# Which engine copies the carry column of a scan tile: ScalarE for two tiles of three instead of one

## The chip, the cores and the metric

The kernel runs on one core of a Trainium2 chip. The core has a matrix engine (TensorE, PE in the profile), three engines for elementwise work (VectorE = DVE, ScalarE = ACT, GpSimd = POOL) and a queue engine (SyncE = SP) that issues its transfers. Each engine works through its own list of instructions in order and waits on semaphores for the others. The metric is the device time of one execution in microseconds (us), lower is better. Before the change it is 11125.21 us, the median of three runs (11121.33 to 11125.94).

## The reference

The input is 8 images of 64 x 64 pixels with 96 channels. Two layers are computed one after the other, each added to its input. The first is a selective scan block: group norm, a projection to 192 channels, a 3x3 depthwise convolution with SiLU, then a recurrence along the 4096 pixels in four directions, and at the end a norm, a gate and an output projection. The second is a small MLP between an upsampling and a downsampling filter. Nearly all of the time goes to the recurrence:

```
def step(h, inp):
    ul, dl, Bl, Cl = inp                       # one pixel
    dA = jnp.exp(dl[..., None] * A)            # 4 directions x 192 channels x 16 states
    h = dA * h + (dl * ul)[..., None] * Bl[:, :, None, :]
    y = jnp.einsum('bkdn,bkn->bkd', h, Cl)
    return (h, y)
_, ys = lax.scan(step, h0, (u_t, d_t, B_t, C_t))
```

## The kernel before, in words

**Tiles.** A tile holds 8 channels x 16 states on the 128 partitions and T = 1024 pixels along the free axis. For an image and a direction k the 4096 pixels are cut into NCH = 4 chunks, and each chunk has NT = 24 tiles, one for each group g of 8 channels. That makes 8 x 4 x 4 x 24 = 3072 tiles. They are worked off in one long loop, chunk after chunk, the 24 groups of a chunk one behind the other.

**A tile's work.** `product_b` (L1069, always GpSimd) forms the input term bb. `decay` (L1071 to L1082) has TensorE spread dl over the states into a PSUM tile pd (four matmul rows of the profile, L1075), and ScalarE takes the exponential of pd in place (L1082). `scan` (L1089, VectorE) runs the recurrence through the tile. `product_c` (L1095) multiplies the result by C, and `sums` (L1127) has TensorE add over the states.

**Thirds.** Tiles are dealt out by i % 3, where i counts the 24 tiles of a chunk. A tile with i % 3 == 2 is "GpSimd's" (`by_pool`): its scan writes to a tile h in SBUF, and GpSimd forms its product. The other two thirds scan in place in PSUM, and VectorE forms their product. In this text tile 0, tile 1 and tile 2 are the tiles of the three residues, and tile 0' is the tile 0 that follows tile 2.

**The carry.** The scan of a chunk starts from the last column of the same group in the chunk before. `hold` (L1104) therefore copies one column of the finished tile (the last one, or the first one for the backward directions) into column g of a small tile `carry`. The last chunk of a direction needs no copy, so three tiles of four have one: 2304 copies in all. Before the change ScalarE copies for tiles 2, from SBUF, and VectorE for tiles 0 and 1, from PSUM.

**Buffers.** pd has two buffers (L232). The matmuls of tile n + 2 therefore wait until everything that reads the pd of tile n is done: its scan alone for a tile 2, its product and its copy for tiles 0 and 1.

**Order.** The order on every engine is written out by hand in the loop: in the step of tile n come the product of tile n - 1 if it is GpSimd's, `product_b` for tile n + 3, `decay` for tile n + 1, the scan of tile n, its product if VectorE's, its copy, then a portion of side work (`side.advance`: the convolutions, norms and the MLP of neighbouring images, rationed by `Side.CAPS`, L49), a filler matmul if PE has little to do (`turn_over`, L1097), and every second step the sums. So on ScalarE the list reads: exp of tile n + 1, copy of tile n if it is ScalarE's, side work, exp of tile n + 2, and so on.

Of the kernel before, what the change touches and what calls it, by code (L numbers as in the profile page):

```python
# [136 lines left out]
def kernel(ctx: ExitStack, tc: tile.TileContext, a: dict, out: bass.AP):  # L137
    nc = tc.nc
# [965 lines left out]
    def hold(t):  # L1104
        if t["last"]:
            return
        end = T - 1 if t["k"] < 2 else 0
        (nc.scalar.copy if t["by_pool"] else nc.vector.tensor_copy)(  # L1108
            carry[:, t["g"] : t["g"] + 1], t["h"][:, end : end + 1]
        )  # L1110

# [60 lines left out]
    with tc.manual_schedule():  # L1172
# [20 lines left out]
        for i in range(n + 4):  # L1193
            t = tiles[i] if i < n else None
# [48 lines left out]
            if t:  # L1243
                scan(t)
                if not t["by_pool"]:
                    product_c(t)
                hold(t)
# [105 lines left out]
```

## Time and profile before

| what | us |
|---|---|
| median of three runs | 11125.21 |
| the profiled execution | 11107.68 |
| its span (first to last instruction) | 11105.8 |
| busy: VectorE / GpSimd / TensorE / ScalarE | 10207.5 / 10179.6 / 9967.9 / 5910.6 |
| stretch 125 to 10835 us, in which the scans run | 10710, VectorE busy 10157.2, GpSimd 10147.7 |
| VectorE's 3072 scans, about 2.3 each | 7164 |
| VectorE's 2048 products (1.225 each), GpSimd's 1024 (2.357 each) | 2508.4 and 2413.9 |
| VectorE's 1536 copies, 0.148 each | 228.0 |
| ScalarE's 768 copies, 0.183 each | 140.8 |

A row of the profile such as "L1108 DVE COPY carry<-pd" names the source line, the engine, the operation and what it writes and reads. Busy times are sums over the rows of one engine; two rows that follow each other closely can overlap by some 0.08 us, since the next instruction starts before the one before has fully ended. A line of the waits names the instruction that waited, what released it, the total in us, the number of times and the longest.

### The profile page before, as it was taken

What the parts mean: (1) busy time and instruction counts of PE and PEld (TensorE: products, weight loads), DVE (VectorE), ACT (ScalarE), POOL (GpSimd) and SP (SyncE); (2) the same over time, 40 slices, a digit from 0 to 9 for tenths busy, and PEclk for the clock granted to TensorE, in tenths of its full rate; (3) what the DMA queues carried; (4) which work ended last, traced back from release to release, by engine and by line L of the source; (5) the groups of instructions that cost most, each with busy time, mean ns of one, the idle gap of its engine ahead of it and who ended that gap; (6) DMA issues with size and microseconds to landing.
All of it is one profiled execution on the core that took longest, in us unless ns stands there. A gap on an engine that the chain in (4) does not pass through costs nothing. (4 is left out here: it accounts for less than half of the span.)

```text
span 11105.8 us, 137238 instructions
## 1 busy us (share of the span) xinstructions
PE 9967.9 (90%) x45020; PEld 3204.6 (29%) x45020; DVE 10207.5 (92%) x7702; ACT 5910.6 (53%) x8218; POOL 10179.6 (92%) x4674
## 2 busy tenths in 40 slices
PE   8898888989889998999889998899988989889988
PEld 2222222322233222332223322233222332223325
DVE  6999999999999999999999999999999999999990
ACT  5455445656455564555545555455554655545543
POOL 5999999999999999999999999999999999999990
PEclk9999999999999999999999999999999999999998
DMA  6888898898988989888988989889898898988981
GB/s 174 215 208 224 209 231 209 217 227 232 233 209 216 225 231 225 212 218 224 240 217 215 224 221 244 209 219 225 217 243 210 217 228 218 247 206 216 227 214 48
DMA packets 1044463, 2401.27 MB, mean 216 GB/s; under 512 B 293820, under 2 KB 314556, under 8 KB 1043752
## 3 DMA queue, kind: packets, MB, share of 16 engines
q1 hardware_dynamic: 1042776, 2391.45, 86.5%
q8 instruction: 361, 5.91, 0.2%
q14 instruction: 350, 2.87, 0.1%
q10 hardware_dynamic: 976, 1.04, 0.0%
HBM read 1929.05 MB, written 328.73 MB: 203 GB/s over the span
## 5 line engine op out<-in xcount | busy, mean ns | idle before, releaser
L1069 POOL TENSOR_TENSOR bb<-dub,br 128x1024 f32<-128x1024 f32 x3072 | 7173.5, 2359 | 208.4 <-DMA dub<-du 149.2
L1082 ACT ACTIVATE pd<-pd,neg_a 128x1024 f32<-128x1024 f32 x3072 | 3340.7, 1088 | 4533.0 <-PE pd L1075 4489.8
L1075 PE MATMUL pd<-dl,sel_b 64*128 64x512 f32 x12288 | 3512.7, 645 | 987.2 <-DVE carry L1108 649.2
L1089 DVE TENSOR_TENSOR_SCAN pd<-pd,carry,bb 128x1024 f32<-128x1024 f32 x1536 | 3610.3, 2350 | 262.2 <-ACT carry L1108 127.9
L1095 POOL TENSOR_TENSOR hc<-h,cr 128x1024 f32<-128x1024 f32 x1024 | 2413.9, 2357 | 352.6 <-DVE h L1089 300.7
L1095 DVE TENSOR_TENSOR hc<-pd,cr 128x1024 f32<-128x1024 f32 x2048 | 2508.4, 1225 | 164.1 <-PE py L1127 20.0
L1075 PEld LDWEIGHTS pd<-dl,sel_b 64*128 64x128 f32 x12288 | 966.7, 186 | 3266.3 <-issue 1511.2
L1089 DVE TENSOR_TENSOR_SCAN h<-pd,carry,bb 128x1024 f32<-128x1024 f32 x768 | 1797.3, 2340 | 5.8 <-ACT pd L1082 5.6
L1127 PE MATMUL py<-hc,sel_r 128*32 128x512 f32 x12288 | 1715.0, 617 | 30.4 <-POOL hc L1095 30.2
L1089 DVE TENSOR_TENSOR_SCAN pd<-pd,bb 128x1024 f32<-128x1024 f32 x512 | 1172.5, 2290 | 98.6 <-ACT carry L1108 75.3
L1101 PE MATMUL idle<-sel_b,ident 128*128 128x512 f32 x1652 | 932.0, 646 | 8.0 <-DVE ty L720 5.9
L562 PE MATMUL pc<-pad,convr 96*128 96x512 f32 (+1 forms) x2304 | 858.3, 616 | 5.7 <-DVE e L585 3.6
L1089 DVE TENSOR_TENSOR_SCAN h<-pd,bb 128x1024 f32<-128x1024 f32 x256 | 583.6, 2280 | 26.0 <-ACT pd L1082 25.2
L1127 PEld LDWEIGHTS py<-hc,sel_r 128*32 128x32 f32 x12288 | 250.3, 109 | 1109.0 <-issue 854.5
L1031 POOL TENSOR_TENSOR u<-dl,u 128x512 f32<-128x512 f32 x384 | 485.0, 1271 | 79.2 <-DVE dl L1028 79.2
L862 PEld LDWEIGHTS p<-w2q,mq 128*100 128x100 f32 x4800 | 452.9, 168 | 274.6 <-issue 214.2
L855 PE MATMUL ph<-xu,w 96*128 96x500 f32 x960 | 504.9, 629 | 11.5 <-ACT mq L856 6.7
L862 PE MATMUL p<-w2q,mq 128*100 128x96 f32 x4800 | 511.5, 258 | 2.3 <-ACT mq L856 2.3
L562 PEld LDWEIGHTS pc<-pad,convr 96*128 96x128 f32 (+1 forms) x2304 | 266.3, 163 | 563.9 <-issue 552.8
L987 PE MATMUL px<-u,xp 64*64 64x512 f32 x1536 | 422.4, 627 | 2.4 <-issue 2.4
L1101 PEld LDWEIGHTS idle<-sel_b,ident 128*128 128x128 f32 x1652 | 249.8, 189 | 596.5 <-issue 522.4
L1012 PE MATMUL pv<-xd,dt_w 64*64 64x512 f32 x1536 | 394.4, 609 | 1.0 <-ACT xd L997 1.0
(153 smaller groups left out, 6707.9 us busy)
## 6 DMA issues: line engine op xcount, KB each, us to landing
dub<-du SPq DMA_DIRECT2D x3072, 512.0 KB
u<-u SPq DMA_DIRECT2D x256, 384.0 KB
du<-u SPq DMA_DIRECT2D x768, 128.0 KB
y<-yq SPq DMA_DIRECT2D x768, 128.0 KB
br<-xd SPq DMA_DIRECT2D x256, 256.0 KB
cr<-xd SPq DMA_DIRECT2D x256, 256.0 KB
yp<-y SPq DMA_DIRECT2D x384, 128.0 KB
yp<-u SPq DMA_DIRECT2D x192, 128.0 KB
```

The lines of the kernel that those rows point to most:

```text
L562: nc.tensor.matmul(t[rows].rearrange("p (i j) -> p i j", i=8), weights[:, cs], v["pad"][:, 8 * blk + kw : 8 * blk + kw + 8, kh : kh + H], ...
L855: nc.tensor.matmul(t[:, :px], w1[:, m, :], xu, start=True, stop=True)
L862: nc.tensor.matmul(t[:SIDE, C * i : C * i + C], sq[:, m, row], w2q[:, m, :], start=(m == 0), stop=(m == 2))
L987: nc.tensor.matmul(p[rows], xp[rows, k, q, :], v["u"][rows, q, :], start=(q == 0), stop=(q == 2), skip_group_check=True,)
L1031: nc.gpsimd.tensor_tensor(v["u"][:, q, :], got["dl"][:, q, :], v["u"][:, q, :], ALU.mult)
L1069: nc.gpsimd.tensor_tensor(t["bb"], t["dub"], t["got"]["br"], ALU.mult)
L1075: nc.tensor.matmul(pd[:, MB * hf : MB * hf + MB], sel_b[rows, 4 * t["s"] + t["j"]].rearrange("p n c -> p (n c)"), t["got"]["dl"][rows, t[" ...
L1082: nc.scalar.activation(pd, pd, AF.Exp, scale=neg_a[:, t["k"], t["g"] : t["g"] + 1])
L1089: nc.vector.tensor_tensor_scan(t["h"][:, ::step], pd[:, ::step], t["bb"][:, ::step], 0.0 if t["first"] else held, ALU.mult, ALU.add)
L1095: (nc.gpsimd if t["by_pool"] else nc.vector).tensor_tensor(t["hc"], t["h"], t["got"]["cr"], ALU.mult)
L1101: nc.tensor.matmul(p, ident, sel_b[:, 0:4].rearrange("p j n c -> p (j n c)"), start=True, stop=True)
L1127: nc.tensor.matmul(py[r0 : r0 + 32], sel_r[:, t["j"], :], t["hc"][:, MB * hf : MB * hf + MB], start=(t["j"] == 0), stop=(t["j"] == 3 and t ...
```

## The change

`hold` chooses its engine by the tile's place instead of by `by_pool`. Tiles 2 stay on ScalarE and tiles 0 on VectorE; the copies of tiles 1 (768 of them), which read pd in PSUM, move from VectorE to ScalarE. The blank line moves all later source lines by one.

```
-        (nc.scalar.copy if t["by_pool"] else nc.vector.tensor_copy)(
+
+        (nc.vector.tensor_copy if t["i"] % 3 == 0 else nc.scalar.copy)(
             carry[:, t["g"] : t["g"] + 1], t["h"][:, end : end + 1]
         )
```

In the list of the changed program's instructions, with the semaphore value that each waits for, three more things differ. The moved copy waits on ScalarE until VectorE has finished `product_c` of tile 1, not only its scan. The matmuls of tile 0' wait for ScalarE's copy where they waited for VectorE's. And the exp of tile 0' has a second wait, for the copy, in 621 of 768 cases behind its wait for the matmuls.

## The prediction

> **What bounds the kernel now.** I read the page's busy times first, then the copy's own rows and who waited for them, then VectorE's waits, then one group of three tiles in order of time. From the page:
>
> ```profile
> PE 9967.9 (90%) x45020; PEld 3204.6 (29%) x45020; DVE 10207.5 (92%) x7702; ACT 5910.6 (53%) x8218; POOL 10179.6 (92%) x4674
> ```
>
> VectorE and GpSimd share the lead, ScalarE is half idle. By that line alone, moving work from VectorE to ScalarE looks free. The rows of line 1108 say who is held up by the copy:
>
> ```profile
> L1108 DVE COPY carry<-pd x1536: 146/148/151, 123.6 to 10750.5; 128x1 f32<-128x1 f32 x192
> L1108 ACT COPY carry<-h x768: 172/182/193, 133.1 to 10754.4; 128x1 f32<-128x1 f32 x192
> ...
>   PE pd L1075: 649.2, 796
> ```
>
> TensorE's decay matmuls waited 796 times for a copy: it stands on the way to releasing a pd buffer. The waits tell which of the two leaders drives:
>
> ```profile
> DVE pd L1089 <- ACT carry L1108: 203.2, 414, 3.6
> ...
> POOL hc L1095 <- DVE h L1089: 300.7, 335, 6.4
> ...
> DVE pd L1089 <- ACT pd L1082: 113.8, 238, 8.0
> ...
> DVE pd L1089 <- POOL bb L1069: 40.2, 38, 2.3
> ```
>
> GpSimd waits 300.7 us for VectorE's scans, VectorE only 40.2 us for GpSimd, so VectorE sets the pace. Its own large waits are before in-place scans, for ScalarE. The line names the copy, but the order of time shows that the exp in front of it is meant (the chain of tiles 1, 2 and 0'):
>
> ```profile
> 5013.53 1.22 DVE L1095 TENSOR_TENSOR hc<-pd,cr 128x1024 f32<-128x1024 f32 x1
> 5014.67 0.15 DVE L1108 COPY carry<-pd 128x1 f32<-128x1 f32 x1
> 5014.74 2.34 DVE L1089 TENSOR_TENSOR_SCAN h<-pd,carry,bb 128x1024 f32<-128x1024 f32 x1
> ...
> 5014.97 1.13 PE L1075 MATMUL pd<-dl,sel_b 64*128 64x512 f32 x4 [1.31 <-DVE carry L1108]
> ...
> 5016.13 1.09 ACT L1082 ACTIVATE pd<-pd,neg_a 128x1024 f32<-128x1024 f32 x1 [2.77 <-PE pd L1075]
> ...
> 5017.15 0.18 ACT L1108 COPY carry<-h 128x1 f32<-128x1 f32 x1
> ...
> 5017.32 2.36 DVE L1089 TENSOR_TENSOR_SCAN pd<-pd,carry,bb 128x1024 f32<-128x1024 f32 x1 [0.24 <-ACT carry L1108]
> ```
>
> Product 1 ends at 5014.75, copy 1 at 5014.82, the matmuls of tile 0' run 5014.97 to 5016.10, its exp to 5017.22, and scan 0' starts 0.10 later. Meanwhile VectorE finished scan 2 at 5017.08 and stood idle. So from product 1 to scan 0' there are two ways: VectorE's own (copy, scan 2) and a chain through TensorE and ScalarE, and the chain is longer by about 0.3 us. Counted over the trace: of the 768 groups of three with copies, 485 have scan 0' starting within 0.13 us of its exp's end. In these the chain decides; in the other 283 side work of VectorE or something else does.
>
> **The change, part by part.** The sum is made for the profiled execution (11107.7 us, span 11105.8) and carried to the median of the runs, which is 17.5 us higher.
>
> *Removed from VectorE:* 768 copies. One does not cost its 0.148: it starts 0.084 before the product's end, and the scan starts 0.083 before the copy's end, where without a copy (tile pairs of the last chunks) the scan starts 0.084 before the product's end. Each costs 0.064, together 49 us. That is the most that can be gained, and only where VectorE's own way is the longer one.
>
> *Added to ScalarE:* 768 copies from PSUM. The row for SBUF is 0.183. ScalarE's 96x1 activations take 0.249 from PSUM (L493) and 0.203 from SBUF (L494), so PSUM adds 0.046; I take 0.230, with 0.183 as the lower end.
>
> *The new wait.* The copy waits for product 1. ScalarE's copies that waited for a scan of VectorE began 0.034 after its end (121 cases). Released are the matmuls of tile 0'. In the chunks without copies, matmuls with a single wait began 0.054 after the product (118 cases); a matmul of L855 that waited for ScalarE began 0.052 after it (12 cases). So product to matmuls takes 0.034 + 0.230 + 0.052 = 0.316. Before, it was 0.210 in the common form with two waits (407 cases) and 0.119 with one (58). Then the exp: with its matmul wait alone or last it follows the matmuls by 0.039 to 0.048, but the exps of tiles 1 that carry a second wait behind it followed by 0.108 (249 cases). 621 exps of tile 0' get this form: +0.069. Together the chain grows by 0.106 + 0.069 = 0.175 us in the common case, 0.13 with the shorter copy.
>
> The Trainium skill, "PSUM — Partial Sum Buffer", section "PSUM bank collisions raise a hardware error", speaks against the change: two engines may not touch one bank and quadrant at the same time, readers included, and the back end orders them. That is a reason why a copy that needs only scan 1 is put behind product 1, which reads the same tile; no row of the trace before shows two engines reading one pd. Were copy and product allowed side by side, the sum would be the first rival's below.
>
> Term 1: of the 485, 412 have no further trouble (next paragraph). I put each exp where the new chain ends and compared with the old start of scan 0'. The mean is 0.150, as some matmuls were late already because of TensorE's own list: **+61.7 us** (+50.0 with the short copy).
>
> *What is queued behind the waiting copy.* ScalarE's list is exp 2, copy 1, side work, exp 0'. Before, the side work could start when exp 2 ended, at the median 1.12 us before product 1's end, and had some 3.6 us. Now it starts after the copy, and exp 0' is ready 0.052 + 1.129 + 0.108 = 1.29 us later. Side work there: median 0.60 us, 90% point 1.90, over 1.3 in 138 of 768 groups (sigmoids L506 to L511, squares L856, the Ln and Exp of L1024 and L1026). With each instruction overlapping the one before by 0.075, the exp is late in 130 groups, by 0.60 at the mean. In 73 of them the chain decided before: +0.73 each with the 0.175 included, 53.3 us. In 57 there was slack: +0.28 each, 16.0 us. Term 2: **+69.3 us** (+63.9).
>
> Term 3: in the remaining 226 groups VectorE's own way decides or the slack swallows the delay: **-10.4 us** (-11.9) by the missing copies.
>
> *Hidden parts.* The second semaphore of scan 0' (for product 1) is met 2.3 us early and costs nothing as long as scan 2 lies between. ScalarE has the time: 53% busy, and 768 x 0.230 is 177 us. Tiles 0 and 2 and their releases stay as they are, and no transfer is issued or moved. GpSimd comes later with VectorE; its 300.7 us of waiting grows.
>
> Sum: 61.7 + 69.3 - 10.4 = **+120.6 us** (+102 with the short copy; +79.7 if the exp's second wait also costs nothing; +153.3 if ScalarE's signal reaches TensorE as slowly as the 0.146 seen in the two-wait form). 11107.7 + 120.6 = 11228 for the profiled run, **11245 us** on the median.
>
> **Rivals.**
> *1. The copy runs beside the product (faster).* Scan 1 ends 1.26 us before product 1. A copy released then is done early, the matmuls follow product 1 by 0.054 instead of 0.210, and VectorE saves 0.064. It decides if copies start before the product's end. Price: 485 x 0.156 + 283 x 0.064 = -94, given back 485 x 0.069 for the second wait: -60, so about 11065. Against it stands the wait in the instruction list.
> *2. The chain alone.* If side work on ScalarE has found its place in other gaps, Term 2 shrinks to the 0.175 for its 73 groups: 61.7 + 12.8 - 10.4 = +64, so 11189. For it: ScalarE is idle 4490 us before exps. Against it: that idle time lies before exp 0' no longer, since the copy cuts it off.
> *3. The late side work spreads.* TensorE's next side matmuls read what ScalarE wrote late, and the matmuls of tile 1' stand behind them; exps of tile 1 have a median slack of 0.73 before their scan. If the overrun of 130 x 0.60 = 77 us is paid once more, the sum is +198 and the time 11323.
> *4. No change.* Stalls of other origin (POOL 40.2 us and TensorE's list) take up the delay and the copy is short: within 22 us of 11125.
>
> **Chances.** Forecast (+80 to +155) 0.60, rival 3 and beyond 0.17, rival 2 0.14, rival 1 0.04, rival 4 0.05. The range takes the forecast, rival 2 and rival 3 to a little beyond its price: 11170 to 11335. About 0.2% (22 us) is what a measurement can tell from no change: faster 0.04, same 0.05, slower 0.91.
>
> **What would show it.** In the profile after: VectorE's copies halved to 768; ScalarE's copies of pd near 0.23 us and released by product 1 (L1095); TensorE's decay matmuls waiting for ScalarE's copy; VectorE's idle time before the in-place scans (262.2 and 98.6 us before) up by 100 or more; ScalarE idle some 700 us before the moved copies (768 x the 0.96 mean between exp 2 and product 1). The prediction is wrong if the moved copies start with the scan's end, if scan 0' is no later after product 1 than now (median 2.78 us), or if side work between copy and exp 0' ends before the matmuls do nearly always.

## The result and the profile after

The changed kernel takes 11188.83 us, median of four runs (11185.53 to 11193.91), against 11123.27 us for the kernel before, also four runs. The ratio is 1.0064, 95% interval 1.0051 to 1.0076: 57 to 85 us slower. The profiled execution took 11193.9 us, 86 us more than that of before. The runs of the kernel before lie between 11088 and 11138 us over the study, so the 66 us of the medians and the 86 us of the profiled pair differ by no more than this scatter. The account by stages below is that of the profiled pair, so it explains 86 us, some 20 us more than the medians show.

The page's busy times after the change, the line that made the move look free:

```profile
PE 10003.0 (89%) x45020; PEld 3195.3 (29%) x45020; DVE 10162.9 (91%) x6934; ACT 5995.3 (54%) x8986; POOL 10188.2 (91%) x4674
```

VectorE lost 44.6 us of busy time, ScalarE gained 84.7. Nothing in this line tells of the 86 us: the added time is waiting. The rows of the copy's line show where (first the rows, then what ScalarE waited for before them, then who waited for them, each with us and times):

```profile
L1109 DVE COPY carry<-pd x768: 148/148/150, 125.6 to 10830.9; 128x1 f32<-128x1 f32 x192
L1109 ACT COPY carry<-pd x768: 159/159/174, 129.9 to 10836.1; 128x1 f32<-128x1 f32 x192
L1109 ACT COPY carry<-h x768: 172/181/211, 133.6 to 10839.8; 128x1 f32<-128x1 f32 x192
...
  DVE hc L1095: 806.6, 750
...
  PEld pd L1075: 973.1, 759
  PE pd L1075: 713.4, 797
```

ScalarE stood idle 806.6 us in front of the moved copies, and what ended it 750 times is the product, not the scan. VectorE's own waits (us, times, longest):

```profile
DVE pd L1089 <- ACT pd L1082: 363.1, 612, 8.0
DVE pd L1089 <- POOL bb L1069: 51.6, 41, 3.4
...
DVE pd L1089 <- issue: 35.2, 40, 2.8
...
DVE pd L1089 <- ACT carry L1109: 23.5, 21, 2.3
```

The waits of in-place scans for ScalarE were 317.0 us under two names before. They are 421.8 us now with the line "issue" added, whose scans all start within 0.13 us of the end of their exp. VectorE's rows of the in-place scans say the same: the number behind the second bar is VectorE's idle time in front of them. First before:

```profile
L1089 DVE TENSOR_TENSOR_SCAN pd<-pd,carry,bb 128x1024 f32<-128x1024 f32 x1536 | 3610.3, 2350 | 262.2 <-ACT carry L1108 127.9 <-ACT pd L1082 91.9 <-POOL bb L1069 39.7
...
L1089 DVE TENSOR_TENSOR_SCAN pd<-pd,bb 128x1024 f32<-128x1024 f32 x512 | 1172.5, 2290 | 98.6 <-ACT carry L1108 75.3 <-ACT pd L1082 21.9 <-POOL bb L1069 0.5
```

and after:

```profile
L1089 DVE TENSOR_TENSOR_SCAN pd<-pd,carry,bb 128x1024 f32<-128x1024 f32 x1536 | 3610.8, 2351 | 364.9 <-ACT pd L1082 248.5 <-POOL bb L1069 47.7 <-issue 31.5
...
L1089 DVE TENSOR_TENSOR_SCAN pd<-pd,bb 128x1024 f32<-128x1024 f32 x512 | 1172.7, 2290 | 124.0 <-ACT pd L1082 114.6 <-POOL bb L1069 3.9 <-issue 3.8
```

Last, one group of three in order of time, one with much side work:

```profile
4397.86 1.23 DVE L1095 TENSOR_TENSOR hc<-pd,cr 128x1024 f32<-128x1024 f32 x1
...
4399.00 2.34 DVE L1089 TENSOR_TENSOR_SCAN h<-pd,carry,bb 128x1024 f32<-128x1024 f32 x1
4399.12 0.16 ACT L1109 COPY carry<-pd 128x1 f32<-128x1 f32 x1 [1.16 <-DVE hc L1095]
4399.18 0.60 ACT L701 ACTIVATE sq<-pm 96x512 f32<-96x512 f32 x1
...
4399.33 1.13 PE L1075 MATMUL pd<-dl,sel_b 64*128 64x512 f32 x4 [0.47 <-ACT carry L1109]
4399.67 0.58 ACT L702 COPY ty<-pm 96x512 f32<-96x512 f32 x1
4400.13 0.61 ACT L701 ACTIVATE sq<-pm 96x512 f32<-96x512 f32 x1
...
4400.62 0.60 ACT L702 COPY ty<-pm 96x512 f32<-96x512 f32 x1
...
4401.09 1.12 ACT L1082 ACTIVATE pd<-pd,neg_a 128x1024 f32<-128x1024 f32 x1
...
4402.30 2.36 DVE L1089 TENSOR_TENSOR_SCAN pd<-pd,carry,bb 128x1024 f32<-128x1024 f32 x1 [0.95 <-ACT carry L1109]
```

Product 1 ends at 4399.09, the copy starts 0.03 later after ScalarE had idled 1.16 us. Four side instructions, which take 2.0 us in all, come behind it; in the list of before, nothing that waits for product 1 stood in front of them. The matmuls of tile 0' are done at 4400.46, but exp 0' begins only when the side work lets go, at 4401.09, and scan 0' starts 0.95 us after VectorE had finished scan 2.

**Where the 86 us lie.** The loop was cut at VectorE's instructions, each stage summed over the trace after less the trace before:

| stretch | us |
|---|---|
| 768 groups with copies: end of product 1 to start of scan 0' | +95.3 |
| of it: end of product 1 to start of scan 2 (the missing copy) | -44.5 |
| of it: start of scan 2 to start of scan 0' | +139.8 |
| the same groups: scan 0' to product 1 | -9.2 |
| the 255 groups without copies | -2.8 |
| ahead of the first scan and behind the last | +2.9 |
| sum | +86.2 |

### The profile page after: what moved, and what is told of

The parts are those of the page before. It is cut to its first block, busy times and chain, and to the rows that moved or that the text cites. A ratio compares the mean times of both kernels' runs of the same rounds, so it can differ in the third digit from the quotient of the medians.

```text
span 11192.1 us, 136447 instructions
## 1 busy us (share of the span) xinstructions
PE 10003.0 (89%) x45020; PEld 3195.3 (29%) x45020; DVE 10162.9 (91%) x6934; ACT 5995.3 (54%) x8986; POOL 10188.2 (91%) x4674
## 3 DMA queue, kind: packets, MB, share of 16 engines
q1 hardware_dynamic: 1042776, 2391.45, 86.2%
q14 instruction: 346, 2.83, 0.1%
## 5 line engine op out<-in xcount | busy, mean ns | idle before, releaser
L1089 DVE TENSOR_TENSOR_SCAN pd<-pd,carry,bb 128x1024 f32<-128x1024 f32 x1536 | 3610.8, 2351 | 364.9 <-ACT pd L1082 248.5
L1095 POOL TENSOR_TENSOR hc<-h,cr 128x1024 f32<-128x1024 f32 x1024 | 2416.1, 2360 | 404.6 <-DVE h L1089 354.3
L1089 DVE TENSOR_TENSOR_SCAN pd<-pd,bb 128x1024 f32<-128x1024 f32 x512 | 1172.7, 2290 | 124.0 <-ACT pd L1082 114.6
L1109 ACT COPY carry<-pd 128x1 f32<-128x1 f32 x768 | 122.5, 160 | 806.7 <-DVE hc L1095 806.6
```

The source lines that it names most:

```text
L1089: nc.vector.tensor_tensor_scan(t["h"][:, ::step], pd[:, ::step], t["bb"][:, ::step], 0.0 if t["first"] else held, ALU.mult, ALU.add)
L1095: (nc.gpsimd if t["by_pool"] else nc.vector).tensor_tensor(t["hc"], t["h"], t["got"]["cr"], ALU.mult)
```

## The experiments

Theory: the copy on ScalarE lengthens the chain product 1, copy, matmuls, exp 0', scan 0', and cuts side work off behind it. Rivals: the chain alone; the queue alone; any copy given to ScalarE; VectorE's own time. Times are medians, with ratios to the kernel before, run beside them.

**1. The copy of tile 1 twice** (edit on the changed kernel):

```
-        (nc.vector.tensor_copy if t["i"] % 3 == 0 else nc.scalar.copy)(
-            carry[...], t["h"][...]
-        )
+        for _ in range(1 + (t["i"] % 3 == 1)):
+            (nc.vector.tensor_copy if t["i"] % 3 == 0 else nc.scalar.copy)(
+                carry[...], t["h"][...]
+            )
```

> The changed kernel with ScalarE's copy of tile 1 made twice; the second waits for the first, so it adds 0.16 to 0.22 us between product 1 and the matmuls of tile 0'. Theory (in some 510 groups the chain through the copy, with or without side work behind it, decides when scan 0' starts): 80 to 115 us slower than the change. Rival (the change costs only by the side work queued behind the copy, in 134 groups): 20 to 30 us slower than the change. Rival (VectorE decides): no difference.

Measured 11264.07 us, ratio 1.0132 (1.0119 to 1.0146): 75 us over the change. The source rows of this kernel's copy, whose line is now 1110:

```profile
L1110 ACT COPY carry<-pd x1536: 159/159/174, 129.5 to 10907.0; 128x1 f32<-128x1 f32 x192
...
  DVE hc L1095: 808.4, 752
```

Twice the copies, but ScalarE's idle time in front of them is the same as with one (806.6). From the end of product 1 to the matmuls of tile 0' the median went from 0.246 to 0.437 us, and 136 exps are late behind side work, about as many as with one copy. So 0.19 us more on the way through the copy, with no more side work late behind it, costs 75 us. That is a little under the theory's range and far over both rivals'.

**2. No side work behind the copy, in a pair** (the same edit on the changed kernel and on the one before):

```
-    CAPS = dict(pe=(2.2, 2.9), ...)
+    CAPS = dict(pe=(2.7, 3.4), ...)
...
+            kept = side.left.get("act", 0.0)
+            if t and t["b"] and i % 3 == 1:
+                side.left["act"] = -Side.CAPS["act"][0]
             side.advance(
...
+            if t and t["b"] and i % 3 == 1:
+                side.left["act"] = min(kept + Side.CAPS["act"][0], Side.CAPS["act"][1])
```

> The changed kernel with the side work of ScalarE kept out of the steps of tiles 1 from the second image on (TensorE's ration is raised from 2.2 to 2.7 so that the side work still comes through). To be compared with the next kernel, which is the kernel before with the same rationing. Theory (of the change's +66 to +86 us, more than half is side work queued behind the copy, the rest the longer chain): with nothing queued there, the difference of the pair shrinks to 20 to 45 us. Rival (all of it is the longer chain): the difference stays at 65 to 90 us. The level of both may differ from the kernels without the rationing.

> The kernel before with the same rationing as the kernel just above: its partner. Of itself, the side work that leaves the steps of tiles 1 crowds the steps of tiles 0 and 2, whose exps have about 0.7 us and 1.1 us to spare: up to 60 us slower than before.

Measured 11521.40 us (1.0370, 1.0355 to 1.0386) and 11471.53 us (1.0322, 1.0301 to 1.0344). The new rationing itself costs far more than expected, 350 us: the stretch from scan 0' to scan 1' grew by 0.3 us a group, so exps of tiles 1 come late. The difference of the pair is 50 us, between the two ranges; going by the outer ends of the two intervals it could be anything from 12 to 95 us, so the times alone decide nothing here. The traces tell more. Exps 0' late behind side work are down to 11 in each kernel, against 134 in the changed kernel and 32 in the one before, so that term is gone. But the chain now decides in 594 groups of the partner in place of 485. 594 x 0.092 us (the chain's growth, below) is 55 us, and the stretch from product 1 to scan 0' differs by 57. The pair fits the theory after the fact; its size was not forecast, and it is no separate proof of the term for side work.

**3. The copy ahead of the product** (on the changed kernel):

```
                 scan(t)
+                if t["i"] % 3 == 1:
+                    hold(t)
                 if not t["by_pool"]:
                     product_c(t)
-                hold(t)
+                if t["i"] % 3 != 1:
+                    hold(t)
```

> The changed kernel with the copy of tile 1 written ahead of its product. Then ScalarE copies as soon as scan 1 is done, and VectorE's product waits for the copy, which stands behind exp 2 on ScalarE. Theory (order on one PSUM tile makes the cost: whoever is second waits): the product comes later by 0.2 to 0.4 us, the matmuls follow it at once; 100 to 250 us slower than before, and the side work behind the copy no longer makes exps late. Rival (the cost is only the side work behind the copy): that is gone, so no slower than before.

Measured 11302.97 us, ratio 1.0173 (1.0158 to 1.0188), in the middle of the theory's range. Now the product waits for the copy, as the first line of VectorE's waits says:

```profile
DVE hc L1095 <- ACT carry L1109: 413.2, 761, 6.8
DVE pd L1089 <- ACT carry L1109: 152.6, 337, 3.8
```

Against the kernel before, the stretch from scan 1 to the end of product 1 grew by 349 us, that from product 1 to scan 0' shrank by 137, and only 7 exps 0' are late behind side work. The queue is cleared and the kernel is slower still: two readers of one pd stand one behind the other, and the first one's own waits are paid by the second.

**4. No copy for tiles 1, no copy for tiles 0** (on the kernel before; the second with `== 0`; a memset of `carry` to zero is added at the start):

```
-        if t["last"]:
+        if t["last"] or t["i"] % 3 == 1:
             return
```

> The kernel before without any copy for tiles 1 (their carry stays zero, so the scans of later chunks start wrong; nothing else is left out). Bounds what the copy of tile 1 can be worth. Theory (chain): matmuls of tile 0' follow product 1 by 0.054 (418 groups with one wait) or 0.146 (350 with two) instead of 0.210; mean gain 0.11 in some 485 groups where the chain decides, 0.064 in the other 283: 60 to 75 us faster than before, about 11055. Rival (VectorE's own time is the price of a copy): 49 us faster, and VectorE's idle time before scans 0' unchanged.

> The kernel before without any copy for tiles 0 (their carry stays zero, so the scans of later chunks start wrong; nothing else is left out). VectorE loses the same 768 copies as where ScalarE copied for tiles 0, but nothing is put on ScalarE. Theory (the gain there was lost to ScalarE's exp 2 and side work held behind the copy): 35 to 55 us faster than before. Rival (whatever VectorE saves ahead of the chain is lost again where the matmuls of tile 0' wait for TensorE's and GpSimd's own lists): 5 to 25 us faster.

Measured 11091.77 us (0.9978, 0.9968 to 0.9988) and 11092.87 us (0.9976, 0.9966 to 0.9986): 24 and 27 us gained by the ratios. Without copy 1, less than half of what was expected: the matmuls follow product 1 by a median 0.147 in place of 0.211, but 357 in place of 303 of them start right behind other work of TensorE, and the exps come 0.02 us later at the mean. Without copy 0, the stretch from scan 0 to scan 1 lost the 47 us that it should, and 20 us come back later: 15 between product 1 and scan 0', 5 between scan 1 and product 1. So about half of what VectorE saves is lost again, in many small pieces; the rival's range for tiles 0, 5 to 25 us, is just missed.

**5. ScalarE for tiles 0 and 2, VectorE for tiles 1** (on the changed kernel):

```
-        (nc.vector.tensor_copy if t["i"] % 3 == 0 else nc.scalar.copy)(
+        (nc.vector.tensor_copy if t["i"] % 3 == 1 else nc.scalar.copy)(
```

> ScalarE copies for tiles 0 and 2, VectorE for tiles 1: the same number of copies moved as in the change, but of the tile whose release feeds exp 2, which was ready a median 1.1 us ahead of scan 2. Theory (what costs is the chain product 1, copy, matmuls, exp 0', scan 0', and the side work cut off behind the copy; a copy taken from VectorE is worth 0.064 us): the longer way of copy 0 is swallowed by that slack, all 768 groups gain the 0.064, less a little where exp 2 is late: 25 to 49 us faster than before, about 11080. Rival (any copy of a pd tile given to ScalarE costs, by ScalarE's blocked list): 40 us or more slower, as in the change.

Measured 11107.22 us, ratio 0.9993 (0.9984 to 1.0002). The rival is refuted: as many copies went to ScalarE as in the change, and nothing is lost. ScalarE idles before these copies nearly as long:

```profile
L1109 ACT COPY carry<-pd x768: 159/159/165, 127.2 to 10746.3; 128x1 f32<-128x1 f32 x192
...
  DVE hc L1095: 651.3, 660
```

148 exps of tiles 2 are late behind side work, but only 87 scans 2 start at their exp's end: the slack of tile 2 takes up the delay, as the theory says. The gain that it promised did not come. The stretch from scan 0 to scan 1 is shorter by 45.5 us, that from product 1 to scan 0' longer by 40.9. Beside number 4, some 20 us of the loss would come with any saving at this place, and some 20 us (0.9993 against 0.9976, with intervals that just overlap) come with ScalarE's copy. The trace shows where most of the 40.9 us lie: the matmuls of tile 0' start 0.434 us after product 1 at the mean, 0.387 before, which is 36 us over 768 groups. Of those that start more than 0.25 us after it (260, 208 before), 125 stand right behind the sums in TensorE's list, 91 before. Why the sums stand in the way more often was not tested by itself; number 8 comes nearest.

**6. All copies on ScalarE** (`nc.scalar.copy(` without a choice, on the changed kernel):

> ScalarE makes all copies, of tiles 0, 1 and 2. Theory: the cost of tile 1 (+66 in the runs, +86 in the profiled pair) and the gain of tile 0 (25 to 49) add up: 15 to 55 us slower than before. Rival (a ScalarE list held up twice in three tiles has no room left for its side work): more than the change itself, over 90 us slower than before.

Measured 11195.82 us, ratio 1.0069 (1.0053 to 1.0084): about the change itself, between the two ranges. Against the change, the stretch from scan 0 to scan 1 is 41 us shorter and that from product 1 to scan 0' 24 us longer, the rest is lost in smaller pieces, and the two profiled executions differ by 1 us. The sum of the parts failed much as in number 5.

**7. Scan 1 to SBUF**, so that pd is free 1.26 us earlier (on the changed kernel):

```
-        t["h"] = sp.tile([128, T], F32, tag="h", name="h", bufs=2) if t["by_pool"] else pd
+        t["h"] = sp.tile([128, T], F32, tag="h", name="h", bufs=2) if t["i"] % 3 else pd
```

> The changed kernel, with the scan of tile 1 written to a tile h in SBUF as that of tile 2 is; VectorE's product and ScalarE's copy read h, and pd is free as soon as scan 1 ends, 1.26 us before the product's end. Theory (the chain product 1, copy, matmuls, exp 0' is what VectorE waits for): most of VectorE's 296 us before scans 0' goes, the copy no longer blocks ScalarE, and GpSimd, TensorE and ScalarE take up a part of the gain: 60 to 200 us faster than before, 10920 to 11060. Rival (GpSimd, 10148 us busy of 10710, is the bound as well): under 40 us. Rival (VectorE's product from two SBUF tiles is slower than the 1.225 us from PSUM, or disturbs GpSimd): slower than before by up to 200 us.

Measured 11977.19 us, ratio 1.0784 (1.0766 to 1.0803). The groups of VectorE by shape:

```profile
L1095 DVE TENSOR_TENSOR hc<-h,cr 128x1024 f32<-128x1024 f32 x1024 | 2471.4, 2414 | 71.6 <-DVE h L1089 0.5
...
L1089 DVE TENSOR_TENSOR_SCAN pd<-pd,carry,bb 128x1024 f32<-128x1024 f32 x768 | 1794.3, 2336 | 73.5 <-ACT carry L1109 43.0
L1095 DVE TENSOR_TENSOR hc<-pd,cr 128x1024 f32<-128x1024 f32 x1024 | 1254.2, 1225 | 73.2 <-PE py L1128 1.9
```

The waits for the chain are much smaller: VectorE is idle 112 us before the scans of tiles 0, of which 73.5 stand in the second row, where it was 324 us before and 458 in the changed kernel. This is no clean test of the theory, because VectorE's own way from scan 1 to scan 0' grew too. The product from two SBUF tiles takes 2.414 us at the mean in place of 1.225, and GpSimd's product_b 2.627 in place of 2.362. 1024 x 1.19 is 1218 us, more than all waits could give. So the last rival came true, with a price of some 860 us, far above its range. The Trainium skill, "SBUF — State Buffer", section "Who interferes with whom", says that a VectorE instruction with two SBUF inputs contends with a GpSimd instruction that reads SBUF. The trace agrees: the shortest such product took 1.224, the median 2.199, and GpSimd's product_b grew as well.

**8. The sums behind the matmuls of tile 0'**, in three kernels (before, the copies of number 5, the changed one):

```
             if i + 1 < n:
                 decay(tiles[i + 1])
+            if i % 2 == 0 and 3 <= i - 1 <= n + 2 and i - 1 < n and i % 3 == 2:
+                add_up(i - 1)
...
-            if ends:
-                sums(tiles[i - 3 : i - 1])
-                if tiles[i - 2]["j"] == 3:
-                    side.stores.append([g := store(tiles[i - 2]), next(g)])
+            if ends and (not t or i % 3 != 1):
+                add_up(i)
```

> The kernel before, with the sums that stand in TensorE's list right ahead of the matmuls of tile 0' (every second group) written behind them. In the profile of before, those matmuls start more than 0.25 us after product 1 in 208 groups, 133 us in all, and 104 us of that with sums right in front. Theory (TensorE's list is what the chain meets besides the copy): 20 to 70 us faster than before. Rival (the sums only move into the way of something else): within 20 us of before, or slower.

> The same move of the sums, with ScalarE copying for tiles 0 and 2 and VectorE for tiles 1. Without the move this exchange of copies gained 8 us of the 45 that it took off VectorE. Theory (the rest went to matmuls of tile 0' late behind sums): 25 to 49 us faster than the kernel just above. Rival (GpSimd, or ScalarE's later exps, take up the rest): within 15 us of it.

> The changed kernel with the same move of the sums. Theory (the change lengthens the chain by 0.09 us in each group where the chain decides and puts side work behind the copy; with fewer matmuls late for the sums, the chain decides no less often): 60 to 100 us slower than the kernel before with the moved sums. Rival (the change's cost comes from its place behind the sums): under 40 us slower than it.

Measured 11451.19 us (1.0295, 1.0281 to 1.0309), 11431.47 us (1.0282, 1.0268 to 1.0296) and 11538.40 us (1.0378, 1.0364 to 1.0393). The first expectation failed badly. The matmuls of tile 0' do come sooner after product 1 (mean 0.300 in place of 0.387), but the sums now stand ahead of those of tile 1', and the stretch from scan 0' to scan 1' grew by 273 us. GpSimd, too, now waits for buffers that the sums release late, a wait that the kernel before does not have (from the first of the three):

```profile
POOL hc L1095 <- PE py L1127: 215.8, 217, 3.1
```

Number 5's copies gain 20 us here by the medians, with intervals that overlap, and the stretch from product 1 to scan 0' is longer with them by 12 us, where it was 40.9 without the move of the sums. That agrees with the sums as the place of number 5's loss, but so rough a change of the order does not prove it. The change costs 87 us in this surrounding too, within the theory's range.

## Why the prediction was right

The time lies inside the range, the sign is right, and the 66 us of the runs are about half of the 121 forecast. The forecast's own band, +80 to +155, holds the 86 us of the profiled pair but not the 66 us of the medians: these are inside the range only because it was drawn wide enough to take in rival 2. By its steps:

- **The new wait** is as read from the instruction list: ScalarE's copies are released by the product. Rival 1 is out, and number 3 shows what an order the other way round costs.
- **The chain's growth was put too high: 0.092 us, not 0.175.** Before, the tightest tenth of the groups took 2.566 us from product 1 to scan 0', after it 2.658. The hops were right: 0.034 + 0.159 + 0.053 = 0.246 to the matmuls, and the exp with its second wait 0.108 behind them. Two terms were off. The copy from PSUM took 0.159 us and not 0.230; I had added a surcharge for PSUM from L493 against L494, which differ by a per-partition bias operand as well; two rows that both have one, L488 from PSUM (0.248) and L489 from SBUF (0.295), show no surcharge (in both pairs the functions differ too). And scan 0' follows its exp by 0.088 in place of 0.102.
- **Term 1** was the most mis-sized: +39.1 us in 408 groups where +61.7 in 412 were forecast; 408 x 0.092 is 37.5.
- **Term 2**: 134 exps late behind side work, by 76.5 us, where 130 and 78 us were forecast; +56.8 us of it at scan 0' against +69.3. Most of the difference is the chain's growth that the term contained: 130 x 0.083, what it was too high by, is 10.8. (32 exps were late before the change too.)
- **Term 3**: -0.5 us, not -10.4. 190 of its 226 groups did save 0.044 us each at the mean (-8.4 us), but in the other 36 the exp now decides, and they lost 7.9.
- **The sum** at scan 0' is +95.3 against +120.6. Carried on in a straight line from the prediction's own two values, 0.230 and 0.183, a copy of 0.159 gives +44, +61 and -13 for the three terms, +92 in all. The mechanism holds and the size of the copy was wrong, but that this sum comes so near is partly luck: its first two terms are still 9 us too high, and its third is 12 us too low. Another -9.2 us came from stretches that the prediction left untouched, which is no more than two runs of one kernel differ by.
- **Carrying to the median** added an error: the profiled execution of before was 17.5 us under its median, that after 5 us over its own. That offset was no property of the kernel.
- **Rival 2**, at 11189, hits the time to the microsecond, by luck, and is wrong all the same: it has late side work cost nothing beyond the chain's growth, 12.8 us, and the 134 groups with late exps paid 57. **Rival 3** did not show in the changed kernel: the stretch from scan 0' to product 1 became no longer.
- **Signs.** VectorE's idle time before in-place scans rose from 262.2 + 98.6 to 364.9 + 124.0 us, by 128; ScalarE's before the moved copies is 806.6 where 700 were expected; GpSimd's wait for scans grew from 300.7 to 354.3. Scan 0' follows product 1 by 2.83 us at the median, 2.78 before.

What stays open: number 4 and 5 show that a saving ahead of the chain is half lost again, and more where ScalarE makes the copy; apart from number 5's matmuls behind the sums, the pieces are small and were not told apart. Each trace is of one execution, so pieces under some 20 us may be scatter. No version that makes all its copies is clearly faster than the kernel before; number 5 is level with it within 0.2%.

## What to carry to other kernels

A half-idle engine is not free for work that must wait: ask what stands behind the moved instruction in its new list, and whom its completion releases. Here 49 us of VectorE time were handed to an engine with 47% to spare, and what came back was a longer chain in two thirds of the groups and side work locked up behind a wait. In this loop, where several engines run near their limit, a delay on the chain that sets the pace was paid for the most part (0.19 us more per copy cost 75 us), while about half of a saving of 47 us on one engine was lost again further on.

## What the runs showed of the hardware

- ScalarE's 128x1 copy took 0.159 us from PSUM and 0.183 us from SBUF; of its 96x1 activations with a bias operand, the one from PSUM was the shorter too: 0.248 (L488) against 0.295 (L489, from SBUF).
- Instructions started later where a second wait stood in the list behind the one that ended last. TensorE's matmuls started 0.055 us after VectorE's product with a single wait, for the product, and 0.147 with a second wait behind it (number 4, no copy for tiles 1). ScalarE's exp started 0.039 to 0.048 us after the matmuls when that wait was alone or the later in the list, and 0.108 with another wait behind it.
- VectorE's product of 128x1024 floats took 1.225 us with one input in PSUM, and 2.414 us at the mean with both in SBUF beside a busy GpSimd.
